# A local transformer's step loop: four quads of heads in flight in place of three, in a new order of phases

## Chip, core and metric

The kernel runs on one core of one Trainium2 chip. The metric is the device time of one launch in microseconds; lower is better. Times before the change are of three runs, and one further execution was profiled.

## What is computed

The reference is a chain of twelve residual blocks on an activation of 8 x 256 tokens by 128 channels, all in float32: expert layers, attentions, a recurrent block, and twice a six-layer local transformer (the reference's `_L2_ffn_ref`). The change touches only that transformer, which is run once before and once after another attention. Its core:

```python
def attn_layer(x, Wqkv, qs, ksc, Wo):           # 16 heads of 64
    q, k, v = split(x @ Wqkv)
    q = l2norm(q) * qs;  k = l2norm(k) * ksc
    q = q * cos * scale + rotate_half(q) * sin * scale
    k = k * cos * inv + rotate_half(k) * sin * inv
    out = local_attention(q, k, v)              # windows of 32, each sees itself and the one before
    return out @ Wo
def ffn_layer(x, g, bln, W1, b1, W2, b2):
    xn = layernorm(x) * g + bln
    a, gate = split(xn @ W1 + b1)
    return a * gelu(gate) @ W2 + b2
for i in range(6):
    x = attn_layer(shift_tokens(x), ...) + x
    x = ffn_layer(shift_tokens(x), ...) + x
```

`shift_tokens` moves the upper half of the channels by one token; `l2norm` divides each head's 64 values by their norm.

## The kernel before

Activations lie transposed, 128 channels on the partitions, in groups of two sequences (`T` = 512 tokens, four groups). The twelve stages follow one another; a local stage is `ffn2` (L1583). A **unit** is one layer for one group, 6 x 4 = 24 in a stage and 48 in the kernel. A unit has 16 heads in four **quads** of four heads, so a stage has 96 quads, and one pass of the loop in `ffn2`, a **step**, takes in one new quad `q0` while the ones of the steps before, `q1` and `q2`, are at later phases. Phases of a quad:

- `quad_project` (L1304): for k and then q, two matmuls into a pair of psum banks (`pp`); ScalarE squares it (`l_sq`), VectorE multiplies it with the sine table (`l_y`) and the cosine table (`l_yk`, `l_yq`); two DMAs swap neighbouring partitions (`l_yr`, L1318).
- `quad_norms` (L1335): the squares' column sums for q and k in one psum bank, four strips of 32 partitions; Ln and Exp on ScalarE give 1/norm (`l_rn`); two DMAs spread the key part over the partitions (`l_sq<-l_rn`, L1353); GpSimd adds the swapped half to k (`l_yk`).
- `quad_values` (L1323): the values (`vp`), copied by ScalarE to `l_v` and by two DMAs into a copy shifted by 32 rows (`l_w`).
- `quad_scale` (L1357): small matmuls turn the query norms into columns (`l_rq`, here called picks), VectorE adds the swapped half to q and multiplies k with its norms into the padded key rows (`l_kp`).
- `quad_scores` (L1376): mask and 64 small score matmuls (`sc`; 128 in the trace[...]), maximum and subtraction on VectorE (`l_mx`, `l_e`), multiplication with the query norms on GpSimd. `quad_exp` is ScalarE's Exp.
- `quad_turn` (L1412): transposes of `l_e`, copied by ScalarE to `l_at`. `quad_weigh` (L1422): two pairs of psum banks (`cx`) of weighted values, divided by VectorE (`l_cx`). `quad_back` and `quad_done`: transposes of `l_cx`, copied by ScalarE to `l_ct`.

When a unit's last quad is done, `local_rest` (L1461) does the remainder in pieces handed out four to a step by `piece`: the output projection in three parts, the residual sum `x1`, its shift `xs` (upper half on ScalarE, lower half on GpSimd), the layer norm, the gate matmuls with Gelu, the second matmul. A new unit's input is shifted the same way at the head of the step of its first quad.

Three things set the order. All instructions of VectorE, ScalarE, GpSimd and TensorE in the stage are forced into program order by `_Ordered` (their rows in the profile therefore all carry L298); DMAs are issued from SyncE. Psum: three pairs go round in turn for everything that `two` gives out, one bank for norms and picks (`bank`), one accumulator (`acc`). The buffers of `l_sq` are two, shared by k's squares, q's squares and the spread norms.

Of the kernel before, what the change touches and what calls it, by code (L numbers as in the profile page):

```python
# [21 lines left out]
F32 = mybir.dt.float32  # L22
# [6 lines left out]
P = 128  # L29
B, S, D = 8, 256, 128  # L30
NB = 2
# [275 lines left out]
class _Net:  # L307
# [98 lines left out]
    def spare(self):  # L406
        return self.bank.tile([P, T], F32, tag="bank", name="bank")

    def norm_parts(self, x, mean="mean", eps=0, gamma=None, beta=None, out=None, own=False):


        bank, tile = (self.ps, self.work) if own else (self.spare, self.scratch)
        m = bank()
        self.mm(m, self.get(mean), x)
        xc = tile("ln_c")
        self.nc.vector.tensor_tensor(xc, x, m, ALU.subtract)
        sq = tile("ln_sq")
        self.nc.scalar.activation(sq, xc, AF.Square)
        yield
        v = bank()  # L420
        self.mm(v, self.get(mean), sq)
        r = tile("ln_r")
        with self.reading(LN_EXP):
            self.rsqrt(r, v, eps, tile=tile)
        y = self.new_x() if out is None else out
        self.nc.vector.tensor_tensor(y, xc, r, ALU.mult)
        if gamma is not None:
            self.nc.vector.tensor_scalar(y, y, gamma, beta, ALU.mult, ALU.add)
        return y
# [871 lines left out]
            out[k] = t.unsqueeze(1).to_broadcast([P, 4, S])  # L1301
        return out

    def quad_project(self, q):  # L1304

        nc = self.nc
        four = lambda a: a.rearrange("p j (b s) -> p (j b) s", b=NB)
        for n, o in (("k", S), ("q", 0)):
            pp = self.two("pp")
            for j in range(2):  # L1310
                self.mm(pp[:, j, :], q.w[:, o + P * j : o + P * (j + 1)], q.xs)
            sq = self.work("l_sq", (P, 2, T), bufs=2)
            nc.scalar.activation(sq, pp, AF.Square)
            y2 = self.work("l_y2", (P, 2, T), bufs=2)
            nc.vector.tensor_tensor(four(y2), four(pp), q.tab[n + "sin"], ALU.mult)
            yr = self.work("l_yr", (P, 2, T), bufs=2)
            for a in range(2):
                nc.sync.dma_start(yr[a::2], y2[1 - a :: 2])  # L1318
            y = self.work("l_y" + n, (P, 2, T), bufs=2)
            nc.vector.tensor_tensor(four(y), four(pp), q.tab[n + "cos"], ALU.mult)  # L1320
            q.y[n], q.yr[n], q.sq[n] = y, yr, sq

    def quad_values(self, q):  # L1323
        nc = self.nc
# [10 lines left out]
    def quad_norms(self, q):  # L1335


        nc = self.nc
        sp = self.ps()
        for s, (n, j) in enumerate((("q", 0), ("q", 1), ("k", 0), ("k", 1))):  # L1340
            to, sq = sp[32 * s : 32 * s + 32, :], q.sq[n][:, j, :]
            if n == "k":
                self.mm(to, self.get("hsum"), sq)
                continue
            for b in range(NB):
                bs = slice(S * b, S * (b + 1))
                self.mm(to[:, bs], self.get("hsum"),
                        sq[:, bs].rearrange("p (c x i) -> p x c i", c=2, x=2))
        q.rn = self.work("l_rn", bufs=2)
        self.rsqrt(q.rn, sp, 2, scale=2.0**SH, shift=3)  # L1350
        q.rk = self.work("l_sq", (P, 2, T), bufs=2)
        for j in range(2):
            nc.sync.dma_start(q.rk[:, j, :], q.rn[64 + 32 * j : 96 + 32 * j, :].unsqueeze(1)  # L1353
                              .to_broadcast([32, 4, T]))
        nc.gpsimd.tensor_tensor(q.y["k"], q.y["k"], q.yr["k"], ALU.add)

    def quad_scale(self, q):  # L1357


        nc = self.nc  # L1360
        tp = self.ps()[:, :16].rearrange("p (m r) -> p m r", r=4)
        for b in range(NB):
            for x in range(2):
                o = S * b + P * x
                self.mm(tp[:, 2 * b + x, :], q.rn[:64, o : o + P], self.get("hpick")[:64, :])
        q.rq = self.work("l_rq", (P, 16), bufs=2)
        nc.vector.tensor_scalar(
            q.rq.rearrange("p (r m) -> p r m", m=4), tp.rearrange("p m r -> p r m"), 1e12, None,
            ALU.min)
        nc.vector.tensor_tensor(q.y["q"], q.y["q"], q.yr["q"], ALU.add)  # L1370
        q.kp = self.kp[q.n % 2]
        nc.vector.scalar_tensor_tensor(
            q.kp[:, :, WIN:], q.rk.rearrange("p j (b s) -> p (j b) s", b=NB), 1e12,
            q.y["k"].rearrange("p j (b s) -> p (j b) s", b=NB), ALU.min, ALU.mult)
# [86 lines left out]
    def local_rest(self, u):  # L1461


        nc, i = self.nc, u.i
        acc = self.accp.tile([P, T], F32, tag="acc", name="wo_acc")

        def project(cs):
            for c in cs:
                self.mm(acc, u.wo[:, c, :], u.ct[c // 2][:, c % 2, :], start=c == 0, stop=c == 7)

        project(range(3))
        yield False
        yield False
        project(range(3, 6))
        yield False
        project(range(6, 8))
        u.x1 = self.new_x()
        nc.vector.tensor_tensor(u.x1, acc, self.ys[u.g], ALU.add)
        xs = self.shifted(u.x1)
        yield False  # L1480

        self.settle()
        norm = self.norm_parts(xs, gamma=self.get(f"F{i}_ln_g"), beta=self.get(f"F{i}_ln_b"),
                               out=self.scratch("t", bufs=2))
        next(norm)
        for _ in range(3):
            yield True
        u.hn = yield from norm
        yield False

        o = self.accp.tile([P, T], F32, tag="acc", name="w2_acc")
        ags = []

        def second(m):
            f = GE_CHUNKS[m][1]
            self.mm(o, u.w2[:f, m, :], ags[m][:f, :], start=m == 0, stop=m == 2)

        def first(m):
            f, w = GE_CHUNKS[m]
            pp = self.two("ge")  # L1500
            self.mm(pp[:w, 0, :], u.w1[:, INNER + f : INNER + f + w], u.hn)
            self.mm(pp[:w, 1, :], u.w1[:, f : f + w], u.hn)
            gl = self.work("l_gl", bufs=2)
            self.act(gl[:w, :], pp[:w, 0, :], AF.Gelu, bias=self.get(f"F{i}_b1", 3 + m, 1)[:w, :])
            ag = self.work("l_ag", bufs=2)
            nc.vector.scalar_tensor_tensor(ag[:w, :], pp[:w, 1, :],
                                           self.get(f"F{i}_b1", m, 1)[:w, :], gl[:w, :],
                                           ALU.add, ALU.mult)
            ags.append(ag)

        self.table("gelu_and_others")
        first(0)
        yield True
        first(1)
        yield True
        second(0)
        yield True
        first(2)
        self.table(LN_EXP)
        second(1)  # L1520
        yield False

        yield False
        yield False
        yield False
        second(2)
        x2 = self.new_x()
        nc.vector.scalar_tensor_tensor(x2, o, self.get(f"F{i}_b2"), u.x1, ALU.add, ALU.add)
        self.ys[u.g] = x2
        if i == DEPTH - 1:  # L1530
            z = self.new_x()
            nc.vector.scalar_tensor_tensor(z, x2, 0.5, self.x[u.g], ALU.mult, ALU.add)
            self.finish(u.g, z)
        yield False
# [48 lines left out]
    def ffn2(self):  # L1583
# [2 lines left out]
        self.table(LN_EXP)  # L1586
        self.ys = [None] * NG
        gen = self.quads()
        q1 = q2 = None
        pieces, left = iter(()), 0  # L1590
        while True:
            q0 = next(gen, None)
            if not (q0 or q1 or q2 or left):
                break
            left = max(left - 1, 0)
            if q2 and q2.last:
                pieces, left = self.local_rest(q2.unit), 3
            if q1:
                self.quad_scores(q1)
            if q0:  # L1600
                self.quad_project(q0)
                if not q0.n:
                    self.window_rows()
            if q1:
                self.quad_exp(q1)
            if q2:
                self.quad_back(q2)
            if q0:
                self.quad_norms(q0)
            if q2:  # L1610
                self.quad_done(q2)
            if q0:
                self.quad_values(q0)
            self.piece(pieces)
            if q1:
                self.quad_turn(q1)
            self.piece(pieces)
            if q0:
                self.quad_scale(q0)
            self.piece(pieces)  # L1620
            if q1:
                self.quad_weigh(q1)
            self.piece(pieces)
            q1, q2 = q0, q1
        self.nc = real


# [136 lines left out]
```

## Time and profile before

| what | us |
|---|---|
| median of three runs | 5755.86 |
| lowest and highest run | 5738.87 and 5764.16 |
| the profiled execution's own time | 5764.6 |
| its span from first to last instruction | 5762.8 |
| local stages in it (960 to 2830, 3175 to 5060) | 3755 |
| TensorE busy in the span | 5194.9 |
| VectorE busy | 3389.1 |
| ScalarE busy | 2447.9 |
| GpSimd busy | 986.3 |

The mean granted TensorE clock of the profiled execution is 0.948 of full speed. In group rows the columns are line, engine, operation, output and inputs, count, then busy us and mean ns, then the engine's idle time just before. Matmuls overlap one another, so their durations do not add up; the distance from one start to the next does. In rows of waits the columns are who waited and for what, total us, number of times, longest. In rows of a stretch of time they are the stretch, its length, busy us of each engine with the number of instructions, the granted clock, the DMA engines' share and GB/s.

### The profile page before, as it was taken

Reading aid. Unit: us, or ns where it says so; the run is one execution under the profiler, and the core shown is the slowest. Engines: PE = TensorE matmul, PEld = TensorE weight load, DVE = VectorE, ACT = ScalarE, POOL = GpSimd, SP = SyncE. Lnnn points to the kernel's source line nnn. Section 1 sums busy time; section 2 is a strip of 40 time slices with the busy share of each in tenths; the row PEclk is TensorE's granted clock in tenths of the full one; section 3 lists DMA queues with packets and bytes.
Section 4 is the critical chain, followed back from the end, with each engine's and each line's share of the span. In section 5 each row is a group of like instructions: output and inputs, shape, how many; then the busy total and the mean of one; then the engine's idle time right before and its main releaser. Section 6 shows DMA issues by size and latency. Waiting matters only on the chain.

```text
span 5762.8 us, 160699 instructions
## 1 busy us (share of the span) xinstructions
PE 5194.9 (90%) x72688; PEld 3146.7 (55%) x72688; DVE 3389.1 (59%) x4903; ACT 2447.9 (42%) x2948; POOL 986.3 (17%) x627
## 2 busy tenths in 40 slices
PE   9989997898999999898888899899999999889889
PEld 6756754555555555555544455555555555555446
DVE  4444455666666666666635666666666666645555
ACT  2233235444444444444434344444444444432342
POOL 0000022222222222222200222222222222200000
PEclk9999988999999999999989899999999999989899
DMA  1000001344443434443300344344444444310000
GB/s 65 1 1 1 1 1 50 101 116 115 114 112 108 127 102 126 109 113 108 98 22 1 101 112 123 104 123 109 123 112 116 118 110 112 100 45 1 1 1 8
DMA packets 171995, 448.39 MB, mean 78 GB/s; under 512 B 26545, under 2 KB 40754, under 8 KB 171058
## 3 DMA queue, kind: packets, MB, share of 16 engines
q1 hardware_dynamic: 171314, 438.12, 27.7%
q8 instruction: 573, 9.39, 0.7%
q14 instruction: 108, 0.88, 0.0%
HBM read 45.51 MB, written 1.05 MB: 8 GB/s over the span
## 4 chain that ended last, share of the span: by engine, by line
PE 68%; ACT 10%; DMA 9%; DVE 8%; issue 4%; POOL 0%; SPq 0%; DVEq 0%; ACTq 0%; POOLq 0%
PE pp L298 14%; PE mm L353 10%; DMA l_sq<-l_rn 9%; PE bank L298 8%; PE e_o L353 6%; PE wo_acc L298 6%; PE ge L298 5%; PE sc L298 4%; ACT l_sq L298 3%; PE vp L298 3%; PE cx L298 3%; PE ms L298 3%; DVE l_kp L298 2%; ACT l_ct L298 2%; PE ss L298 2%
## 5 line engine op out<-in xcount | busy, mean ns | idle before, releaser
L298 ACT ACTIVATE l_sq<-pp 128x1024 f32<-128x1024 f32 x384 | 393.5, 1025 | 1106.2 <-PE pp L298 1106.2
L298 PE MATMUL pp<-l_xs,wqkv 128*128 128x512 f32 x1536 | 789.9, 661 | 11.1 <-ACT l_xs L298 6.6
L298 POOL TENSOR_TENSOR l_e<-l_e,l_rq 128x1024 f32<-128x1024 f32 x192 | 365.6, 1904 | 1881.1 <-DVE l_e L298 1705.7
L298 POOL TENSOR_TENSOR l_yk<-l_yk,l_yr 128x1024 f32<-128x1024 f32 x192 | 452.6, 2357 | 615.6 <-DMA l_yr<-l_y 571.5
L298 PE MATMUL sc<-l_kp,l_yq 64*32 64x64 f32 x24576 | 329.7, 247 | 222.4 <-DVE l_kp L298 200.0
L298 PEld LDWEIGHTS pp<-l_xs,wqkv 128*128 128x128 f32 x1536 | 309.6, 213 | 362.8 <-issue 337.3
L353 PE MATMUL mm<-x,m 128*128 128x512 f32 x1024 | 479.1, 608 | 0.0
L298 PEld LDWEIGHTS sc<-l_kp,l_yq 64*32 64x32 f32 x24576 | 284.0, 115 | 284.4 <-DVE l_kp L298 225.4
L298 DVE SCALAR_TENSOR_TENSOR l_kp<-l_sq,l_yk 128x1024 f32<-128x1024 f32 x192 | 234.7, 1222 | 307.7 <-DMA l_sq<-l_rn 307.5
L353 PEld LDWEIGHTS e_o<-m,e_h 128*128 128x128 f32 x3072 | 362.9, 192 | 60.6 <-issue 60.1
L298 PE MATMUL vp<-wqkv,l_xs 128*128 128x256 f32 x1536 | 382.4, 392 | 1.8 <-PE bank L298 1.1
L298 PE MATMUL wo_acc<-l_ct,wo 128*128 128x512 f32 x768 | 365.3, 609 | 0.0
L353 PE MATMUL e_o<-m,e_h 128*128 128x128 f32 x3072 | 363.5, 275 | 0.0
L298 PEld LDWEIGHTS vp<-wqkv,l_xs 128*128 128x128 f32 x1536 | 276.0, 189 | 114.9 <-issue 77.7
L298 PE MATMUL cx<-l_w,l_at 64*32 64x65 f32 x12288 | 285.5, 228 | 47.1 <-ACT l_at L298 39.3
L298 DVE TENSOR_TENSOR l_y<-pp,l_ksin 128x1024 f32<-128x1024 f32 x192 | 234.8, 1223 | 154.6 <-ACT l_sq L298 154.4
L298 PEld LDWEIGHTS cx<-l_w,l_at 64*32 64x32 f32 x12288 | 251.7, 106 | 129.6 <-issue 80.2
L298 DVE TENSOR_REDUCE l_mx<-sc 128x16 f32<-128x1024 f32 x192 | 234.5, 1221 | 121.6 <-PE sc L298 120.2
L298 PE MATMUL cx<-l_v,l_at 64*32 64x65 f32 x12288 | 290.4, 228 | 11.5 <-issue 11.5
L353 PEld LDWEIGHTS mm<-x,m 128*128 128x128 f32 x1024 | 190.0, 195 | 197.5 <-issue 170.7
L298 PE MATMUL ge<-t,w 128*128 128x512 f32 (+1 forms) x576 | 281.3, 612 | 12.6 <-DVE t L298 5.7
L298 ACT ACTIVATE lv<-bank,sb_c 128x512 f32<-128x512 f32 x268 | 183.8, 686 | 239.1 <-PE bank L298 233.7
(277 smaller groups left out, 9202.4 us busy)
## 6 DMA issues: line engine op xcount, KB each, us to landing
l_yr<-l_y SPq DMA_DIRECT2D x768, 256.0 KB, 2.4
l_sq<-l_rn SPq DMA_DIRECT2D x384, 256.0 KB, 4.3
l_w<-l_v SPq DMA_DIRECT2D x192, 390.0 KB, 6.3
wqkv<-in_f_wqkv SPq DMA_DIRECT2D x48, 384.0 KB, 4.5
l_w<-l_v SPq DMA_DIRECT2D x192, 65.0 KB, 5.5
wo<-in_f_wo SPq DMA_DIRECT2D x12, 512.0 KB, 3.3
m<-in_m_w SPq DMA_DIRECT2D x16, 256.0 KB, 5.4
w<-in_f_w SPq DMA_DIRECT2D x12, 341.0 KB, 2.8
```

The lines of the kernel that those rows point to most:

```text
L298: r = f(*args, **kw)
L353: self.nc.tensor.matmul(out, lhsT=lhsT, rhs=rhs, start=start, stop=stop)
```

## The change

A fourth quad, `q3`, is in flight: the context is turned back and copied a step after it was weighed. `quad_scale` becomes `quad_keys` and runs at the head of the step after the quad's norms. The phases of a step stand in a new order, k's and q's projections are called apart, and the four places of a piece lie elsewhere. The query norms are taken on the tokens' own order, and the picks put them into window order with twice as many matmuls of half the columns. The layer norm inside `local_rest` uses the accumulator's bank, and the pieces are spread anew.

| order in a step | |
|---|---|
| before | scores q1, project k and q q0, exp q1, back q2, norms q0, done q2, values q0, piece, turn q1, piece, scale q0, piece, weigh q1, piece |
| after | keys q1, project k q0, exp q2, project q q0, piece, turn q2, back and done q3, weigh q2, piece, norms q0, piece, scores q1, values q0, piece |

```diff
     def quad_norms(self, q):
...
         for s, (n, j) in enumerate((("q", 0), ("q", 1), ("k", 0), ("k", 1))):
-            to, sq = sp[32 * s : 32 * s + 32, :], q.sq[n][:, j, :]
-            if n == "k":
-                self.mm(to, self.get("hsum"), sq)
-                continue
-            for b in range(NB):
-                bs = slice(S * b, S * (b + 1))
-                self.mm(to[:, bs], self.get("hsum"),
-                        sq[:, bs].rearrange("p (c x i) -> p x c i", c=2, x=2))
+            self.mm(sp[32 * s : 32 * s + 32, :], self.get("hsum"), q.sq[n][:, j, :])
...
-    def quad_scale(self, q):
+    def quad_keys(self, q):
...
             for x in range(2):
-                o = S * b + P * x
-                self.mm(tp[:, 2 * b + x, :], q.rn[:64, o : o + P], self.get("hpick")[:64, :])
+                for c in range(2):
+                    o = S * b + P * c + 64 * x
+                    self.mm(tp[64 * c : 64 * c + 64, 2 * b + x, :], q.rn[:64, o : o + 64],
+                            self.get("hpick")[:64, :])
...
     def local_rest(self, u):
...
         project(range(3))
         yield False
-        yield False
         project(range(3, 6))
         yield False
+        yield False
+
         project(range(6, 8))
         u.x1 = self.new_x()
         nc.vector.tensor_tensor(u.x1, acc, self.ys[u.g], ALU.add)
         xs = self.shifted(u.x1)
         yield False
-
+        yield False
         self.settle()
         norm = self.norm_parts(xs, gamma=self.get(f"F{i}_ln_g"), beta=self.get(f"F{i}_ln_b"),
-                               out=self.scratch("t", bufs=2))
+                               out=self.scratch("t", bufs=2), bank=self.bank1)
         next(norm)
-        for _ in range(3):
-            yield True
+        yield True
+        yield True
+
         u.hn = yield from norm
         yield False
+        yield False
...
         self.table("gelu_and_others")
         first(0)
-        yield True
         first(1)
-        yield True
-        second(0)
         yield True
         first(2)
         self.table(LN_EXP)
+        second(0)
         second(1)
         yield False
 
-        yield False
-        yield False
-        yield False
         second(2)
...
     def ffn2(self):
...
+            if q1:
+                self.quad_keys(q1)
+            if q0:
+                self.quad_project(q0, "k")
+                if not q0.n:
+                    self.window_rows()
+            if q2:
+                self.quad_exp(q2)
+            if q0:
+                self.quad_project(q0, "q")
+            self.piece(pieces)
+            if q2:
+                self.quad_turn(q2)
+            if q3:
+                self.quad_back(q3)
+                self.quad_done(q3)
+                if q3.last:
+                    pieces, left = self.local_rest(q3.unit), 4
+            if q2:
+                self.quad_weigh(q2)
+            self.piece(pieces)
+            if q0:
+                self.quad_norms(q0)
+            self.piece(pieces)
             if q1:
                 self.quad_scores(q1)
             if q0:
...
                 self.quad_values(q0)
             self.piece(pieces)
...
-            q1, q2 = q0, q1
+            q1, q2, q3 = q0, q1, q2
```

## What I predicted before seeing the result

> **What bounds the kernel now.** I read the page first: TensorE is busy 90% of the span, but its clock row shows 8s and 9s, and the chain that ended last holds 9% of a DMA, the key norms' broadcast.
>
> ```profile
> span 5762.8 us, 160699 instructions
> PE 5194.9 (90%) x72688; PEld 3146.7 (55%) x72688; DVE 3389.1 (59%) x4903; ACT 2447.9 (42%) x2948; POOL 986.3 (17%) x627
> PEclk9999988999999999999989899999999999989899
> PE pp L298 14%; PE mm L353 10%; DMA l_sq<-l_rn 9%; PE bank L298 8%; PE e_o L353 6%; PE wo_acc L298 6%; PE ge L298 5%; PE sc L298 4%; ACT l_sq L298 3%; PE vp L298 3%; PE cx L298 3%; PE ms L298 3%; DVE l_kp L298 2%; ACT l_ct L298 2%; PE ss L298 2%
> ```
>
> Then the stage windows of the two local stages, the only ones touched:
>
> ```profile
> 960.00:2830.00 1870.00, 1677.50 (x29593) 1010.49 (x29592) 1185.68 (x1433) 862.97 (x996) 429.12 (x245) 0.94 0.41 113
> 3175.00:5060.00 1885.00, 1688.24 (x30500) 1024.51 (x30498) 1207.01 (x1461) 873.44 (x1003) 436.44 (x244) 0.96 0.42 113
> ```
>
> Columns are length, busy PE, PEld, DVE, ACT, POOL, granted clock. They make 3755 us for 48 units of four steps: 78.2 us a unit. TensorE idles 192.5 + 196.8 = 389 us, 8.1 a unit. The clock is granted at 1.00 or 0.50, so a mean of 0.94 and 0.96 is half clock for 12% and 8%: 375 us; half of that is lost, 3.9 a unit.
>
> Then the chain in order of time, for one step:
>
> ```profile
> 2043.92 1.03 ACT l_sq L298
> 2044.99 1.16 PE bank L298 x8
> ...
> 2046.23 0.70 ACT lv L298
> ...
> 2048.68 5.81 DMA l_sq<-l_rn
> ...
> 2054.58 1.22 DVE l_kp L298
> ```
>
> Within one step: square, norm matmuls, Ln, Exp, broadcast DMA, scaled keys; then the scores can start. From the norms' end to the keys takes 8.3 to 9.5 us in eight steps of ten (2046.07 to 2054.58 here). The waits name it, and two waits on residual sums of which the change moves one:
>
> ```profile
> PE sc L298 <- DVE l_kp L298: 200.0, 85, 3.9
> DVE l_kp L298 <- DMA l_sq<-l_rn: 307.5, 132, 4.0
> POOL l_xs L298 <- DVE x L298: 461.4, 48, 23.1
> ACT l_xs L298 <- DVE x L298: 311.3, 48, 6.8
> ```
>
> **The change, part by part.** I lay TensorE's matmuls of one step end to end, start to start, at full clock: picks 0.98, k and q projections 3.51, turns of e 0.87, turns of context 0.88, weigh 1.42, norms 1.0, scores with mask 1.73, values 1.83: 12.2. Pieces per unit: Wo 16 x 0.43, two norm means 0.86 each, gate and up 12 x 0.45, W2 6 x 0.49: 16.9. A unit is 4 x 12.2 + 16.9 = 65.9, and 65.9 + 8.1 + 3.9 = 77.9 meets the 78.2. The change leaves this work nearly alone, so all turns on idle time and clock.
>
> *What it removes.* Keys wait a step, so the chain above leaves the scores: up to 200 us. The norm matmuls no longer wait for the squares (about 0.24 a step, 46 us).
>
> *What it puts there.* Three psum pairs go round, each step takes eight (k, q, turned e, turned context, weigh 0 and 1, scores, values), so weigh 0 needs q's pair back, read last by DVE. This is the timeline of DVE from k's square on:
>
> ```profile
> 2043.26 1.22 DVE L298 TENSOR_TENSOR l_y<-pp,l_ksin 128x1024 f32<-128x1024 f32 x1 [0.49 <-ACT l_sq L298]
> 2044.40 1.21 DVE L298 TENSOR_TENSOR l_yk<-pp,l_kcos 128x1024 f32<-128x1024 f32 x1
> 2045.53 1.21 DVE L298 TENSOR_TENSOR l_y<-pp,l_qsin 128x1024 f32<-128x1024 f32 x1
> 2046.66 1.21 DVE L298 TENSOR_TENSOR l_yq<-pp,l_qcos 128x1024 f32<-128x1024 f32 x1
> ```
>
> k's projection starts at 2040.18, q's pair is free at 2047.87: 7.7 us. Before, TensorE filled them with q, context turns, norms and values. Now only projections (3.5) and two turns (1.75) lie there, so weigh starts 1.0 + 7.7 = 8.7 into the step (idle 2.4, less a piece), and 1.42 + 1.0 + 1.73 + 1.83 = 6.0 follow: 14.7 plus later pieces. A unit's four steps I call A (Wo), B (sum and mean), C (variance and gate), D (last W2):
>
> - D: 14.7; TensorE work 13.2, idle 1.5.
> - A: D has no piece after its norms, so D's norms end 3.6 us before A starts. Keys start 8.3 after that (the quick end, the swaps having landed), at 4.75; the four DVE reads queue behind them at 1.13 spacing, q's pair is free at 10.5, weigh starts there: 10.5 + 6.0 + 5.14 of Wo = 21.7; work 17.4, idle 4.3.
> - B: the sum x1 (0.69) stands behind yq on DVE and ends at 9.3; the ACT half of the shift (0.61) waits for it with l_at (1.0) queued behind, so weigh starts at 11.0: 11.0 + 6.0 + 0.86 = 17.85; work 14.8, idle 3.05. Before, this shift ended a step, with nothing urgent behind it.
> - C: a new unit's input shift heads the step, and its POOL half stands behind the score multiply of B, now late in its step: scores end 1.8 before C starts, then max 1.25, subtraction 1.22, multiply 1.90, shift 0.60 on POOL: projections start at 3.5 and not 1.0. 14.7 + 2.5 + 7.4 of pieces = 24.6; work 20.5, idle 4.1.
>
> Idle: 4.3 + 3.05 + 4.1 + 1.5 = 12.95 against 8.1.
>
> *Clock.* Half clock comes in stretches of 3.41 us; the first row is the stretch before one, the second the slow one:
>
> ```profile
> 2014.67:2018.08 3.41, 1.05 (x89) 0.89 (x96) 2.97 (x6) 0.00 (x0) 0.00 (x0) 1.00 0.38 105
> 2018.08:2021.49 3.41, 3.41 (x67) 1.79 (x51) 2.97 (x3) 0.00 (x0) 0.00 (x0) 0.50 0.02 5
> ```
>
> 2.36 us of idle there were enough. Over both stages every such stretch with 2 us idle or more was followed by a slow one, few below 1.4. [...] By the trace, A's gaps (2.1 and 1.4 with turns between) trip it nearly always, B's 2.95 in three of four, C's 2.5 in six of ten, at 1 to 2 us each: 3.65 a unit, as much as before. I take the trace: 65.9 + 12.95 + 3.65 = 82.5.
>
> *Picks, eight matmuls where four were (16 against 8 in the trace).* Before: 8 in 0.98, 188 ns a load of 128 columns. Halves load 64 columns into two column groups; the weigh row runs 128 small ones in 1.42. From below 0.5, from above 1.96 if each costs as before[...]. I take 1.0 (half the columns, twice the count); 1.96 adds about 1 in B and D, +94 us; 0.5 gives -48.
>
> *At nothing.* Query norm matmuls on 512 columns: same columns, 1.0 (0.9 to 1.07). Norms' means in the accumulator bank: wo, mean, variance, w2 follow one another anyhow. Exp moved ahead of q's square on ACT: 1.06, with q's DVE reads not due before (their slack 0.6 before; 0.15 now); if it is late, q's pair is late with it. Gelu pieces pulled together: the table loads (1.28) lie beside 7.4 us of TensorE work. DMAs: k's swap, q's swap, norm broadcast, values keep their order on SP; values' copy has two steps of slack; the broadcast now leaves before the value copy and after the swaps landed, so 7.6 (the least seen) to 9.5: -34 to +58 us. POOL's key add has a step. One step more to drain: some 5 us a stage.
>
> **Sum.** (82.5 - 78.2) x 48 = +206 on the profiled execution's 5764.6, which lies 8.7 over the median of the runs: 5755.9 + 206 = 5962, said as 5960.
>
> **Rivals.**
> 1. *Slower, as above*: chance 0.60; own range 5860 to 6080 (picks, broadcast, clock 2 to 5.5 a unit).
> 2. *Faster*: A's, B's and C's three queue waits are hidden, since one of the orders is not what I read. Idle is then 2.45 + 0.75 + 1.6 + 1.5 = 6.3, no stretch trips the clock often (1.0): 73.2, -5.0 x 48 = -240: 5515; with one of the waits left some 5620. For it: 200 us of score waits do go. Against: each wait is an in-order queue. Chance 0.22. It turns where the three waits fall from 6.7 to 2.4 us a unit.
> 3. *A wash*: the same waits, but gaps broken by the turns keep the clock up: +31, 5785; a wait less, 5730. Chance 0.08 within 0.5%.
> 4. *Slower still*: slow stretches feed themselves (after a slow one, 0.5 us idle kept it slow more often than not) and the picks cost double: 6 a unit of clock and +2: 5962 + 113 + 94 = 6170. Chance 0.10.
>
> A measurement of this kernel tells about 0.5%. So faster 0.22, same 0.08, slower 0.70. The range 5610 to 6080 takes in rival 3 and the near end of rival 2; rival 4's end and the best of rival 2 stay out.
>
> **What would show it.** Right: waits of PE sc for l_kp gone; PE cx waiting for DVE l_yq and for ACT l_at; PE pp waiting for POOL l_xs some 2.5 us in 46 steps or so; DVE l_kp still waiting for the broadcast in one step of four; TensorE idle near 620 us in the local stages at a clock of 0.93 to 0.96. Wrong: weigh starting within 7 us of a step's start, projections never waiting for the shift, or a clock of 0.99.

## The result, and the profile after

| | before | after |
|---|---|---|
| median of the runs, us | 5755.59 (5738.87 to 5764.16, 4 runs) | 6125.86 (6124.63 to 6129.66, 4 runs) |
| span of the profiled execution, us | 5762.8 | 6127.7 |
| mean granted TensorE clock | 0.948 | 0.932 |

The time after is 1.0648 times that before, with a 95% interval of 1.0624 to 1.0673: 370 us more. The direction was forecast and the size was not: +206 was expected, and the result lies above the range of 5610 to 6080.

These are four lines of the page of the changed kernel: span, busy times, the clock in 40 slices, and the chain that ended last by line.

```profile
span 6127.7 us, 162271 instructions
PE 5232.1 (85%) x73456; PEld 3059.9 (50%) x73456; DVE 3698.7 (60%) x4903; ACT 2467.4 (40%) x2947; POOL 1079.8 (18%) x627
PEclk9999988998999998999989899999999999899999
PE mm L353 9%; PE pp L298 8%; PE bank L298 7%; PE e_o L353 6%; PE sc L298 6%; PE ge L298 4%; PE wo_acc L298 4%; DVE l_y L298 4%; PE cx L298 4%; DVE l_yq L298 3%; DVE l_mx L298 2%; DVE l_yk L298 2%; DVE l_e L298 2%; PE ms L298 2%; POOL l_e L298 2%
```

The broadcast of the key norms, 9% of the chain before, is gone from its costliest lines (all DMAs together are 1% of the chain now). In its place stand VectorE lines that were not among them: `l_y`, `l_yq`, `l_mx`, `l_yk`, `l_e`. VectorE runs the same 4903 instructions in 310 us more busy time, which no step of the prediction has.

These are the stage windows again, of the kernel before and then of the changed one, drawn so that they hold both local stages whole. The two shown with the prediction ended 106 and 43 us before the stages did, so its 78.2 us a unit was too low: read from step to step, a unit took 79.0.

```profile
964.00:2936.00 1972.00, 1760.38 (x30720) 1055.79 (x30720) 1229.93 (x1493) 903.13 (x1045) 440.74 (x245) 0.94 0.40 109
3174.00:5103.00 1929.00, 1720.50 (x30688) 1039.77 (x30688) 1217.44 (x1477) 886.75 (x1021) 439.05 (x248) 0.95 0.41 110
```

```profile
964.00:3118.00 2154.00, 1774.61 (x31103) 1010.13 (x31104) 1379.57 (x1493) 913.22 (x1045) 490.46 (x245) 0.92 0.35 100
3362.00:5467.00 2105.00, 1742.21 (x31071) 998.11 (x31072) 1376.79 (x1477) 897.29 (x1019) 482.32 (x248) 0.93 0.35 101
```

The stages grew from 3901 to 4259 us: 358 of the 365 us by which the span grew. TensorE's idle time in them went from 420 to 742 us (+322). The clock records show it at half clock for 417 us before and 647 us after. TensorE was at work in 354 and 523 us of these, and half of that is lost (the projections' matmuls start 429 ns apart at full clock and 853 ns at half): 177 and 262 us (+85). What is left, 3304 and 3255 us, is work at full clock (-49). The forecast had +233 of idle, -12 of clock and no saving; these make 221, and its 206 comes of taking off 78.2 a unit where its own terms for before made 77.9. The forecast took half of all half-clock time as lost, idle time within it included; counted so, the clock's part is +115.

Read by the type of step, from the first pick of one step to that of the next, means in us (they move by up to 0.3 with the number of steps left out at a stage's ends):

| step | predicted at full clock | measured length | idle, predicted | idle, measured | time at half clock |
|---|---|---|---|---|---|
| D | 14.7 | 16.4 | 1.5 | 2.3 | 1.0 |
| A | 21.7 | 21.2 | 4.3 | 2.6 | 1.0 |
| B | 17.85 | 20.8 | 3.05 | 4.0 | 4.55 |
| C | 24.6 | 28.0 | 4.1 | 5.7 | 5.3 |
| a unit | 78.85, with clock 82.5 | 86.4 | 12.95 | 14.6 | 11.8 (9.7 of it at work, so 4.9 lost) |

Taken in the same way, a unit before was 78.95 with 7.85 of idle and 6.9 at half clock (3.0 lost). Most of the clock loss sits in B and C, the two steps in which a shift waits.

The longest waits of TensorE and one of VectorE, in the changed kernel ("issue" is time in which the engine waited for nothing that the profile shows):

```profile
PE pp L298 <- POOL l_xs L298: 194.1, 47, 4.8
...
PE cx L298 <- ACT l_at L298: 186.2, 95, 3.4
...
PE ct L298 <- DVE l_yk L298: 92.8, 91, 2.3
...
PE cx L298 <- issue: 55.5, 59, 1.9
...
DVE l_kp L298 <- DMA l_sq<-l_rn: 24.7, 35, 3.3
```

No row of PE sc waiting for `l_kp` is left. The two costliest rows are the two shifts that the prediction named: the input shift ahead of the projections (4.1 us each, where 2.5 was forecast) and `l_at`, which stands on ScalarE behind the shift of `x1` (155.6 of the 186.2 us fall in the 47 steps B).

Why 4.1 and not 2.5 is seen in three groups, of the kernel before and then of the changed one:

```profile
L298 POOL TENSOR_TENSOR l_e<-l_e,l_rq 128x1024 f32<-128x1024 f32 x192 | 365.6, 1904 | 1881.1 <-DVE l_e L298 1705.7
...
L298 DVE TENSOR_TENSOR l_yq<-l_yq,l_yr 128x1024 f32<-128x1024 f32 x192 | 234.9, 1223 | 2.3 <-DMA l_yr<-l_y 2.3
...
L298 DVE SCALAR_TENSOR_TENSOR l_kp<-l_sq,l_yk 128x1024 f32<-128x1024 f32 x192 | 234.7, 1222 | 307.7 <-DMA l_sq<-l_rn 307.5
```

```profile
L298 POOL TENSOR_TENSOR l_e<-l_e,l_rq 128x1024 f32<-128x1024 f32 x192 | 417.6, 2175 | 1623.5 <-DVE l_e L298 1410.0
...
L298 DVE TENSOR_TENSOR l_yq<-l_yq,l_yr 128x1024 f32<-128x1024 f32 x192 | 364.6, 1899 | 1.3 <-issue 1.1
...
L298 DVE SCALAR_TENSOR_TENSOR l_kp<-l_sq,l_yk 128x1024 f32<-128x1024 f32 x192 | 299.2, 1559 | 25.2 <-DMA l_sq<-l_rn 24.7
```

They now run at the same time. The timeline of VectorE and then of GpSimd at the head of one step C (start, duration) shows what happens:

```profile
2258.94 1.22 DVE L298 TENSOR_TENSOR l_yq<-l_yq,l_yr 128x1024 f32<-128x1024 f32 x1
2260.70 2.30 DVE L298 SCALAR_TENSOR_TENSOR l_kp<-l_sq,l_yk 128x1024 f32<-128x1024 f32 x1 [0.54 <-DMA l_sq<-l_rn]
```

```profile
2259.01 2.91 POOL L298 TENSOR_TENSOR l_e<-l_e,l_rq 128x1024 f32<-128x1024 f32 x1 [7.51 <-DVE l_e L298]
2261.86 1.60 POOL L298 COPY l_xs<-x 64x512 f32<-64x512 f32 x1
```

The query sum starts first and runs at its own 1.22 us; the score multiply beside it takes 2.91, which is 1.0 more than alone. Then the keys start under the multiply and take 2.30, ending some 1.1 us after it; and the shift that starts behind the multiply ends 0.46 us after the keys do, and takes 1.60 where 0.61 is its time alone. Each time the later one ends as if it had stood until the earlier one was done; this is the exclusion spoken of below. It is so throughout: the 136 query sums and key scalings that start under the multiply or the shift end 1.08 to 1.20 us after it, however much of it was left; the 52 multiplies and 36 shifts that come second end 1.76 and 0.47 us after the VectorE instruction. The next two rows are the windows of this step's head and of what follows:

```profile
2258.17:2263.50 5.33, 0.63 (x17) 0.54 (x16) 4.28 (x4) 1.62 (x2) 4.46 (x2) 0.99 0.51 133
2263.50:2268.70 5.20, 5.18 (x9) 2.31 (x10) 0.50 (x1) 1.53 (x2) 0.00 (x0) 0.69 0.00 0
```

TensorE does its picks (0.6 us), stands for 4.7 us, and then runs 5.2 us at a mean clock of 0.69. The wait is paid once as idle time, and again as 1.6 us of lost clock (0.31 of 5.2).

### The profile page after: what moved, and what is told of

Read it like the earlier page. It is cut to its first block, busy times and chain, and to the rows that moved or that the text cites. A ratio compares the mean times of both kernels' runs of the same rounds, so it can differ in the third digit from the quotient of the medians.

```text
span 6127.7 us, 162271 instructions
## 1 busy us (share of the span) xinstructions
PE 5232.1 (85%) x73456; PEld 3059.9 (50%) x73456; DVE 3698.7 (60%) x4903; ACT 2467.4 (40%) x2947; POOL 1079.8 (18%) x627
## 3 DMA queue, kind: packets, MB, share of 16 engines
q1 hardware_dynamic: 171314, 438.12, 24.7%
## 4 chain that ended last, share of the span: by engine, by line
PE 61%; DVE 22%; ACT 7%; issue 6%; POOL 3%; DMA 1%; SPq 0%; DVEq 0%; POOLq 0%; ACTq 0%
PE mm L353 9%; PE pp L298 8%; PE bank L298 7%; PE e_o L353 6%; PE sc L298 6%; PE ge L298 4%; PE wo_acc L298 4%; DVE l_y L298 4%; PE cx L298 4%; DVE l_yq L298 3%; DVE l_mx L298 2%; DVE l_yk L298 2%; DVE l_e L298 2%; PE ms L298 2%; POOL l_e L298 2%
## 5 line engine op out<-in xcount | busy, mean ns | idle before, releaser
L298 POOL TENSOR_TENSOR l_e<-l_e,l_rq 128x1024 f32<-128x1024 f32 x192 | 417.6, 2175 | 1623.5 <-DVE l_e L298 1410.0
L298 PE MATMUL cx<-l_w,l_at 64*32 64x65 f32 x12288 | 346.7, 245 | 244.3 <-ACT l_at L298 186.2
L298 ACT COPY l_v<-vp 128x1024 f32<-128x1024 f32 x192 | 194.4, 1012 | 635.9 <-PE vp L298 565.9
L298 PEld LDWEIGHTS cx<-l_w,l_at 64*32 64x32 f32 x12288 | 278.5, 115 | 308.0 <-ACT l_at L298 216.0
L298 ACT ACTIVATE lv<-bank,sb_c 128x512 f32<-128x512 f32 x221 | 151.9, 687 | 685.4 <-PE bank L298 685.4
L298 PE MATMUL cx<-l_v,l_at 64*32 64x65 f32 x12288 | 354.6, 245 | 24.6 <-issue 24.6
L298 DVE TENSOR_TENSOR l_yq<-l_yq,l_yr 128x1024 f32<-128x1024 f32 x192 | 364.6, 1899 | 1.3 <-issue 1.1
L298 PE MATMUL sc<-l_kp,l_yq 64*32 64x64 f32 x24576 | 302.8, 227 | 34.3 <-issue 34.3
L298 DVE SCALAR_TENSOR_TENSOR l_kp<-l_sq,l_yk 128x1024 f32<-128x1024 f32 x192 | 299.2, 1559 | 25.2 <-DMA l_sq<-l_rn 24.7
L298 PE MATMUL ct<-sb_c,l_cx 128*128 128x128 f32 x1536 | 218.5, 289 | 102.6 <-DVE l_yk L298 92.8
```

The lines of the kernel that those rows point to most:

```text
L298: r = f(*args, **kw)
```

## The experiments

All ratios are to the kernel before, run beside it on the same chip. Differences in us from the changed kernel are between medians taken on different chips; the medians of the kernel before on these lie between 5751 and 5760 us. The letter Q in the expectations is the theory that a queue order (an instruction standing behind another on its engine) sets the loss; the other theories are named there.

**1. The input shift of a new unit, one step earlier.** This is the changed kernel with the shift issued before the last quad of the unit ahead of it is handed out, so that it has the rest of a step to finish. A fourth `l_xs` buffer is needed, for which the tables lose their second one; what that costs by itself was not run.

```diff
-        self.xs = [one("l_xs", i, (P, T)) for i in range(3)]
+        self.xs = [one("l_xs", i, (P, T)) for i in range(4)]
...
-            t = self.work("l_" + k, (P, S), bufs=2)
+            t = self.work("l_" + k, (P, S), bufs=1)
...
-                xs = self.shifted(self.ys[g])
+                xs = self.unit_input(i, g) if (i, g) == (0, 0) else ahead
...
+                    if c == 3 and i * NG + g + 1 < DEPTH * NG:
+                        ahead = self.unit_input(*divmod(i * NG + g + 1, NG))
                     yield q
```

> The changed kernel, but a new unit's input is shifted one step earlier (a fourth l_xs buffer; the table tiles get one buffer each to make room). Theory Q (waits in in-order queues, my prediction's C term): the projections' wait for POOL l_xs, 194 us in 47 steps, goes, and the slow clock that follows it; step C falls from 28.0 to about 22.5 us, 48 x 5.5 = -260: about 5870 us. Rival R (the rotation of three psum pairs is the bound): the wait reappears at weigh as a wait for q's pair, C falls by 2 at most: about 6030 us.

Measured: 5938.4 us (5934.07 to 5945.37), ratio 1.0316 [1.0296, 1.0337], 187 us under the changed kernel. The group of the projections no longer waits for it:

```profile
L298 PE MATMUL pp<-l_xs,wqkv 128*128 128x512 f32 x1536 | 715.4, 609 | 4.3 <-DMA wqkv<-in_f_wqkv 3.1 <-POOL l_xs L298 1.1 <-issue 0.2
```

Step C fell from 28.0 to 23.9 us, and half clock from 11.8 to 8.1 us a unit. No wait at weigh came in its place in C, but a shorter one did: the context's turns wait for `l_yk`, the reader of k's psum pair, 46 times there and 1.5 us each, where they hardly did in the changed kernel. So the rival named above is right in part: a third of the wait comes back at the psum pairs, without the slow clock.

**2. The sum `x1` and its shift, one place earlier.** They now stand at the last place of A instead of the first of B, so nothing urgent is queued behind them on ScalarE.

```diff
         project(range(3, 6))
         yield False
-        yield False
 
         project(range(6, 8))
...
         yield False
         yield False
+        yield False
         self.settle()
```

> The changed kernel, but the third part of the output projection with x1 and its shift stands at the last place of step A in place of the first of step B. Theory Q (B term): the wait of weigh for l_at behind the shift, about 2.4 us in step B, goes, and most of that step's 4.5 us of slow clock; 48 x 3.5 = -170: about 5955 us. Rival R: weigh waits for q's pair at nearly the same point, 48 x 1 = -50: about 6075 us.

Measured: 5945.83 us (5943.0 to 5949.07), ratio 1.0328 [1.0309, 1.0348], 180 us under the changed kernel. The row of waits for `l_at` falls from 186.2 us in 95 to:

```profile
PE cx L298 <- ACT l_at L298: 36.7, 51, 3.0
```

B fell from 20.8 to 15.4 us, while A took over its piece (21.2 to 23.0); B's half clock went from 4.55 to 0.08 us.

**3. Both at once.** The edits of 1 and 2 together.

> The changed kernel with both earlier edits: a new unit's input shifted a step earlier, and x1 with its shift at the last place of step A. If the two waits are separate queues, the gains add: 6126 - 188 - 180 = about 5758 us. If they share one cause (q's psum pair behind them, or the clock), less than three quarters of the sum comes: above 5850 us.

Measured: 5757.82 us (5749.4 to 5763.12, 12 runs), ratio 0.9997 [0.9985, 1.0009]. The two effects add up (187 + 180 = 367; 368 measured), and the net loss is gone: a unit is 78.6 us with 9.4 of idle and 3 at half clock. So two places in the queues cost as much as the whole change loses, and what else it gains and costs comes out even. VectorE and GpSimd still exclude each other here (the multiply takes 2.19 us, the shift 1.53).

**4. Small query-norm matmuls alone, on the kernel before.** Only the query norms as single matmuls, and the halved picks.

```diff
-            to, sq = sp[32 * s : 32 * s + 32, :], q.sq[n][:, j, :]
...
+            self.mm(sp[32 * s : 32 * s + 32, :], self.get("hsum"), q.sq[n][:, j, :])
...
-                self.mm(tp[:, 2 * b + x, :], q.rn[:64, o : o + P], self.get("hpick")[:64, :])
+                for c in range(2):
+                    o = S * b + P * c + 64 * x
+                    self.mm(tp[64 * c : 64 * c + 64, 2 * b + x, :], q.rn[:64, o : o + 64],
+                            self.get("hpick")[:64, :])
```

> The kernel before, with the small query-norm matmuls alone. Picks fall from 0.98 to about 0.6 us. If that counts only where TensorE is the bound (two steps of four): 96 x 0.4 = -40: about 5715 us. If the chain of the key norms hides it all: 5750 us. If the small matmuls cost TensorE more than they save: above 5770 us.

Measured: 5776.06 us (5766.08 to 5786.31, 10 runs), ratio 1.0037 [1.0024, 1.0049]. The long steps get shorter, but the time does not follow. The four kinds of step before were 24.2, 15.9, 23.3 and 15.6 us; now the two long ones, full of TensorE work, are 23.1 and 22.3, and the two short ones, which have few pieces to fill them, 17.2 and 16.9. The wait for the keys did shrink (from 200.0 to 146.4 us), but weigh waits more (on issue 112.3 us for 19.3, on `l_at` 76.7 for 39.3). Half clock rose from 6.9 to 9.8 us a unit. What goes with the waits on issue is said under experiment 9.

**5. Keys between the projections: an attempt to part VectorE from GpSimd.** VectorE's two instructions of the keys step, the query sum and the key scaling, go behind k's two reads, so that they no longer meet the score multiply.

```diff
+    def quad_keys_sum(self, q):
...
         nc.vector.tensor_tensor(q.y["q"], q.y["q"], q.yr["q"], ALU.add)
...
                 self.quad_exp(q2)
+            if q1:
+                self.quad_keys_sum(q1)
             if q0:
                 self.quad_project(q0, "q")
```

> The changed kernel, but VectorE's two sums of the keys step (q with its swapped half, k with its norms) run after k's two reads of psum and before q's. Theory S (VectorE instructions with two SBUF inputs and GpSimd exclude each other at the head of the step): the l_yq sum falls from 1.90 to 1.22 us, l_kp from 1.56 to 1.22, the score multiply from 2.18 to 1.90, the projections' wait for POOL l_xs from 4.1 to about 2.5 us, and A's broadcast wait goes: about 6000 us. Rival: the slow instructions lie beside other work and q's pair is free no sooner: 6100 to 6130 us.

Measured: 6581.15 us (6578.43 to 6582.63), ratio 1.1431 [1.141, 1.1452]: 455 us slower than the changed kernel, which neither theory expected. The parting itself worked: `l_yq` takes 1216 ns, `l_e` 1913, and the projections wait for the shift 2.7 us each time (127.3 us in 47), the size that the prediction had. But the spread norms that the keys read lie in one of `l_sq`'s two buffers. While they wait there, q's square has no buffer, and everything behind it on VectorE waits. Two waits and one row of ScalarE's timeline of this kernel:

```profile
DVE l_y L298 <- ACT l_sq L298: 904.0, 382, 7.5
...
PE cx L298 <- ACT l_at L298: 763.9, 190, 6.8
```

```profile
2529.71 1.02 ACT L298 ACTIVATE l_sq<-pp 128x1024 f32<-128x1024 f32 x1 [3.79 <-issue]
```

**6. The same with a buffer of its own for the spread norms.** Beside the edit of 5 (the tables lose their second buffer here too):

```diff
-        q.rk = self.work("l_sq", (P, 2, T), bufs=2)
+        q.rk = self.work("l_rk", (P, 2, T), bufs=1)
```

> The changed kernel with both sums of the keys step between k's and q's reads, as in the run that took 6581 us, but the spread key norms have a buffer of their own and do not share l_sq's two. If that run was slow because q's square waits for l_kp to free the shared buffer, and l_at and weigh stand behind it: q's reads are still 2.3 us later than in the changed kernel, the exclusion is gone: 6150 to 6300 us. If the shared buffer plays no part: about 6580 us.

Measured: 6028.13 us (6025.17 to 6041.61), ratio 1.0486 [1.0458, 1.0515], 553 us under experiment 5. The shared buffer was what had cost there. What is left still delays q's reads: `l_at` holds weigh for 273.4 us (97 times).

**7. The query sum alone moved away from the score multiply.** It goes into the quad's own norms phase, after weigh, where GpSimd is not in the multiply.

```diff
         nc.gpsimd.tensor_tensor(q.y["k"], q.y["k"], q.yr["k"], ALU.add)
+        nc.vector.tensor_tensor(q.y["q"], q.y["q"], q.yr["q"], ALU.add)
...
     def quad_keys(self, q):
...
-        nc.vector.tensor_tensor(q.y["q"], q.y["q"], q.yr["q"], ALU.add)
```

> The changed kernel, but VectorE's sum of q with its swapped half runs in the quad's own norms phase, after the weighing of the step and not at the head of the next; no buffer or wait of another instruction changes. Theory S (VectorE with two SBUF inputs and GpSimd exclude each other): the sum falls from 1.90 to about 1.22 us, the score multiply from 2.18 towards 1.9, the projections' wait for POOL l_xs from 4.1 to about 3 us: 48 x 1.1 plus some slow clock, about 6050 us. Rival: the exclusion lies beside other work: 6110 to 6140 us.

Measured: 5968.32 us (5950.9 to 5994.29), ratio 1.037 [1.0325, 1.0415], 158 us under the changed kernel: twice what was expected. Both groups are nearly at their own lengths again, though the keys now start under the multiply more often (1782 ns):

```profile
L298 DVE TENSOR_TENSOR l_yq<-l_yq,l_yr 128x1024 f32<-128x1024 f32 x192 | 239.2, 1246 | 80.9 <-DMA l_yr<-l_y 80.7
...
L298 POOL TENSOR_TENSOR l_e<-l_e,l_rq 128x1024 f32<-128x1024 f32 x192 | 367.3, 1913 | 1601.8 <-DVE l_e L298 1293.6 <-DVE l_rq L298 234.7 <-ACT l_v L298 31.1
```

The wait of the projections for the shift fell from 4.1 to 3.4 us (158.2 in 47), and A, B and C each got about 1 us shorter. But the move also takes 1.2 us out of the head of VectorE's queue, so this run alone does not say whether the exclusion or the shorter queue gave the 158 us.

**8. A stand-in in the place of the sum.** Beside the edit of 7, an instruction of the same length that reads psum stands where the query sum had been: the older quad's subtraction once more, into a buffer that nothing reads (for which the tables lose their second one).

```diff
+        if old:
+            stand_in = self.work("l_in", (P, 2 * T), bufs=1)
+            nc.vector.tensor_tensor(stand_in.rearrange("p (n k) -> p n k", k=64), old.sv, old.mx,
+                                    ALU.subtract)
         q.kp = self.kp[q.n % len(self.kp)]
...
-                self.quad_keys(q1)
+                self.quad_keys(q1, q2)
```

> The changed kernel with the query sum moved as in the run before (158 us gained), and in its old place at the head of VectorE's row an instruction of the same length that reads psum (the subtraction of the older quad's scores once more, into a buffer that nothing reads). VectorE's queue is then as long as in the changed kernel, but nothing at that place has both operands in SBUF. Theory X (the gain came from the score multiply on GpSimd no longer meeting the sum): most of the gain stays, 5970 to 6020, the multiply at about 1.9 us, the projections' wait for the shift near 3.4 us. Theory L (it came from a row of VectorE that is one instruction of 1.2 us shorter ahead of the psum reads): the gain is gone, 6100 to 6140, whatever the multiply takes. Between them both have a part, in proportion.

Measured: 5953.1 us (5938.92 to 5962.15), ratio 1.035 [1.033, 1.0369]: 173 us under the changed kernel, with VectorE's queue as long as in it. So the gain does not come from a shorter queue; it comes from what stands beside GpSimd's multiply. The groups of this kernel:

```profile
L298 POOL TENSOR_TENSOR l_e<-l_e,l_rq 128x1024 f32<-128x1024 f32 x192 | 365.3, 1903 | 1589.2 <-DVE l_e L298 1542.5 <-ACT l_gl L298 27.3 <-ACT l_v L298 19.5
...
L298 DVE SCALAR_TENSOR_TENSOR l_kp<-l_sq,l_yk 128x1024 f32<-128x1024 f32 x192 | 289.6, 1508 | 42.1 <-DMA l_sq<-l_rn 35.1 <-POOL l_e L298 5.2 <-issue 0.5
...
L298 DVE TENSOR_TENSOR l_in<-sc,l_mx 128x1024 f32<-128x1024 f32 x190 | 230.7, 1214 | 0.0
```

The stand-in reads psum and takes 1214 ns beside the multiply, which takes its own 1903. It even puts the keys off until the multiply is nearly done (1508 ns in place of 1782 in experiment 7).

**9. Norms and a piece ahead of weigh.** A test of the pair wait: if weigh waits for a psum pair, work put ahead of it should fill the wait.

```diff
-            if q2:
-                self.quad_weigh(q2)
-            self.piece(pieces)
             if q0:
                 self.quad_norms(q0)
             self.piece(pieces)
+            if q2:
+                self.quad_weigh(q2)
+            self.piece(pieces)
             if q1:
                 self.quad_scores(q1)
```

> The changed kernel, but the norms of q0 and the piece after weigh stand ahead of weigh. Theory Q (A term and the pair): the norm matmuls (1.0 us) fill the wait for q's psum pair, and the spread norms leave about 2.4 us earlier, so A's wait of VectorE l_kp for the broadcast goes: 1 us in most steps and 1.5 in A, 192 x 0.8 + 48 x 1 = -200: about 5925 us. Rival (VectorE is the bound of the front half, whatever TensorE does there): 6080 to 6130 us.

Measured: 6089.5 us (6075.01 to 6102.07), ratio 1.0579 [1.0548, 1.061]: 36 us gained where some 200 were expected. The waits at weigh did shrink (`l_at` from 186.2 to 109.9 us), but the scores now often follow weigh directly, and stop within their run for a cause that the profile calls issue:

```profile
PE sc L298 <- issue: 129.0, 102, 3.4
```

It was 34.3 us in 45 in the changed kernel and 22.2 in 31 before. Of the 129 us, 103 fall in the 49 steps in which the scores follow weigh directly. The DMA records show what goes with these stops. This is the row of one queue in the page of the changed kernel (packets, MB, share of the DMA engines' time):

```profile
q8 instruction: 578, 9.47, 0.6%
```

Its packets are of 16 KB. Of the 102 stops of experiment 9, 101 end between 1.2 and 1.6 us after such a packet, and so do all 45 of the changed kernel's; of moments taken at random 5% do, and of weigh's 174 waits with a named releaser in the changed kernel none. Weigh's waits on issue go with these packets as well (59 of 59 in the changed kernel, 44 of 48 in experiment 4). Why TensorE stops there was not shown, and no run varied it by itself.

**10. Experiments 1, 2 and 9 together, with the query sum behind weigh.**

> The changed kernel with all four edits: input shift a step earlier, x1 and shift at the last place of A, norms ahead of weigh, q's sum after weigh. If the waits are separate and the slow clock goes with them: 65 us of TensorE work a unit plus some 6 idle and 2 of clock, 48 x (73 - 79) = -290 against before: about 5470 us. If only the two tested waits can be had: about 5750 us.

Measured: 5779.84 us (5755.53 to 5793.26, 20 runs), ratio 1.0032 [1.0019, 1.0045], where 5470 was expected. With the two shift waits gone the order of experiment 9 gains nothing and costs: issue in the scores rises to 163.7 us in 122 waits, 121 of which end behind a packet of that queue as above. It is 1.7% slower than experiment 11, in which norms and weigh keep their order.

**11. Experiments 1, 2 and 7 together.**

> The changed kernel with three edits: input shift a step earlier, x1 with its shift at the last place of A, q's sum in the norms phase after weigh. If the exclusion between VectorE and GpSimd cost time only through the projections' wait for the input shift, which the first edit has taken away, nothing more comes: about 5758 us. If it also lengthens VectorE's queue at the head of the other steps (A fell by 0.85 and B by 1.2 us with that edit alone): 48 x 2 = -96: about 5660 us.

Measured: 5673.42 us (5671.46 to 5684.5, 4 runs), ratio 0.9866 [0.9844, 0.9888]. This version beats the changed kernel and, by 1.3%, the one before. By the ratios it is also 1.3% (some 75 us) under experiment 3, which holds everything but the moved sum. So what the exclusion costs lies in part at other places than the two shifts; the price of the shifts (367 us) and that of the exclusion (158 us with the shifts in place) overlap and must not be added. Lines of its page, its windows of the first local stage, and its group of the query sum:

```profile
span 5673.4 us, 162200 instructions
PE 5073.1 (89%) x73456; PEld 2986.1 (53%) x73456; DVE 3558.8 (63%) x4903; ACT 2461.7 (43%) x2947; POOL 1039.2 (18%) x629
```

```profile
964.00:2892.00 1928.00, 1691.63 (x31107) 972.44 (x31108) 1313.74 (x1497) 911.06 (x1046) 473.14 (x247) 0.98 0.39 112
```

```profile
L298 DVE TENSOR_TENSOR l_yq<-l_yq,l_yr 128x1024 f32<-128x1024 f32 x192 | 240.6, 1253 | 113.1 <-DMA l_yr<-l_y 112.7
```

A unit is 76.9 us, with 8.3 of idle and 1.8 at half clock; the clock in the stage is 0.98 where it was 0.94 before. The two kernels idle about as long (7.85 before), but here in shorter pieces: gaps of 2 us and more make 0.6 us of a unit's idle time, where they made 3.7 before, and the time at half clock fell from 6.9 to 1.8 us.

**12. The new quad's values between q's projection and the turns, on top of 11.** It was meant to fill what is left of the wait before weigh.

```diff
                 self.quad_project(q0, "q")
+            if q0:
+                self.quad_values(q0)
...
                 self.quad_scores(q1)
-            if q0:
-                self.quad_values(q0)
```

> The kernel of the three edits, but the values' matmuls (1.83 us) stand between q's projection and the turn of e, where TensorE waits for psum pairs. If they fill that wait: 1 us a step, -190 against the three edits: about 5500 us. If the scores, now last in their step, make Exp late at the head of the next (sum, maximum, multiply and Exp are 5.5 us), or Exp and the copies queue up: no better than the three edits, 5660 to 5800 us.

Measured: 6601.28 us (6593.28 to 6608.89), ratio 1.1475 [1.145, 1.15]. The values have two buffers, and in this order the new quad's are written into the ones that weigh is about to read; so this kernel weighs the newer quad's values, and weigh waits for that step's own shifted copy. Its row of waits:

```profile
PE cx L298 <- DMA l_w<-l_v: 695.0, 184, 5.5
```

It says nothing of whether the wait could be filled; that stays open.

## Why the prediction was right, and where it was wrong

*Right: which waits go and which come.* The scores' wait for the keys is gone. Weigh waits for `l_at` behind the shift of `x1`, and the projections for GpSimd's half of the input shift (47 times; 46 were forecast). Experiments 1 to 3 show that these two cost as much as the net loss: with both shifts moved, 0.9997.

*B: right in kind, under-sized.* Weigh waits behind the shift of `x1` as foreseen, in 47 of 48 steps. But B idles 4.0 us for 3.05 (3.3 with the query sum moved, so most of the miss is the exclusion), and its clock was taken at 1 to 2 us in three cases of four and cost 2.0.

*C: under-sized.* The step "scores end, then max 1.25, subtraction 1.22, multiply 1.90, shift 0.60 on POOL: projections start at 3.5" took the durations of before. In the changed order VectorE's query sum and key scaling stand just where the multiply and the shift run, and they exclude each other: the multiply took 2.91 and the shift 1.60 in the step shown, and the wait was 4.1 us in place of 2.5. The idle time of C was 5.7, not 4.1. Experiments 7 and 8 show the exclusion and its price: with the sum moved away from the multiply the kernel gains 158 us, and with a psum-reading instruction put in its place it still gains 173. Experiments 5 and 6, in which the keys do not meet the multiply, give the wait as 2.7 us.

The step did not ask what the two engines do to each other side by side. The trace of before had hardly a case of it (6 of 192 query sums met a GpSimd instruction, the longest for 0.33 us, and no key scaling did), so nothing in its mean durations warned. In the changed kernel 132 of 192 query sums meet one (2.21 us where the others take 1.22), and 56 of the key scalings (2.40 against 1.21). VectorE instructions that read psum kept their 1.21 us beside GpSimd (109 of q's 192 cosine products met one). The view to take for a moved instruction is what GpSimd does at its new place, and not its mean in the old one.

*The clock: under-sized, the largest single term, and put in the wrong steps.* The step "3.65, as much as before" expected A to trip it in nine cases of ten. A, with turns between its gaps, spent only 1.0 us at half clock. B and C, each with one wait of 3 to 5 us, took 4.55 and 5.3. In the forecast's own count, half of all half-clock time, 5.9 us a unit were lost in place of 3.65. What it read from the trace of before (all 46 full-clock stretches of 3.41 us with 2.0 us of idle and more were followed by one at half clock, and 4 of the 932 with less than 1.4) held: in the changed kernel's stages all 81 with 2.0 us and more were followed by one at half clock, half of the 88 with 1.4 to 2.0 us, and none of the 888 with less; after a slow one, 0.6 us of idle kept it slow in 62 cases of 63.

*A: over-sized.* The step "keys start 8.3 after that" let the broadcast set the keys in one step of four. They waited for it 35 times, 24.7 us in all; weigh started 8.5 us into A where 10.5 was forecast, and the idle time was 2.6 us in place of 4.3.

*D and the pair wait: at another place.* The sign "PE cx waiting for DVE l_yq" did not come: no row of waits shows it. The wait for a psum pair stands one phase earlier, where the context's turns wait for k's reader `l_yk` (92.8 us in 91, in A and B). Weigh's second pair waits for ScalarE's `l_ct` (24.6 us in 79) and on issue (55.5 us in 59). D came out at 16.4 for 14.7; the waits on issue in its scores and weigh, some 1.0 us a step, were not foreseen.

*The picks: cheaper than taken.* Taken as 1.0, they measured 0.56 us in place of 0.98 a step, close to the lower end 0.5. The upper end of 1.96, each at its price of before, was far off. But as experiment 4 shows, that saving with the single norm matmuls makes the kernel before 0.4% slower.

*The sum.* Between forecast and result lie 159 us (365 against 206). In the forecast's own terms, a unit idled 1.65 us more than taken and lost 2.25 us more of clock, which for 48 units is 187 us; the base of 78.2 in place of 78.95 takes 36 of them back, and some 8 are left to the stages' ends. In that count its work of 65.9 us came out (86.4 - 14.6 - 5.9), while for the unit before its terms had made 77.9 where 78.95 was measured. The exclusion alone is of the right size for the whole miss: 158 and 173 us by experiments 7 and 8, its idle time and the clock that this costs taken together. With it out the kernel takes 5968 and 5953 us, where 5960 was forecast. But the terms still differ there (in experiment 7 idle 12.15 for 12.95, clock 4.5 for 3.65), so that the misses nearly cancel is luck and not foresight. The range had reached to 5.5 us of clock a unit, but not to that together with longer waits. In the rivals, "slower still" came near the size (6170) with one reason right (6 a unit of clock) and one wrong (double picks).

## What to carry to other kernels

Before moving an instruction on VectorE or GpSimd, look at what the other of the two does at the new place: here two instructions with all operands in SBUF took 2.2 to 2.9 us where 1.2 to 1.9 is their own time. A small copy that others wait for (here a shift of 0.6 us) belongs a place before the long instructions of its queue: two such copies cost as much as the whole 6.5% loss, and two small edits and a buffer undid it. And price an idle gap at its length plus half of the busy half-clock time that follows it: in the step C shown, 4.7 us of idle and 1.6 us of lost clock.

## What the runs showed of the hardware that I had not expected

- The exclusion of VectorE and GpSimd (multiplies of 1.90 us that came second took 2.80 to 2.98): it also acts on a small GpSimd copy (1.60 us in place of 0.61), the one of the two that starts first keeps its own time (1.22 us for the sum, 1.90 for the multiply), and a VectorE instruction that reads psum is free of it (1214 ns beside a multiply of 1903).
- TensorE: 16 picks that each load 64 columns took 0.56 us in the changed kernel, 35 ns each, where 8 that load 128 columns took 0.98 before.
- Where the scores' 128 small float32 matmuls follow weigh's 128 directly, they stop within their run: 103 us in 49 steps of experiment 9. In all, the scores stop for 129.0 us in 102 waits there and for 163.7 in 122 in experiment 10. 101 and 121 of these stops end 1.2 to 1.6 us after a packet of the queue `q8`; the cause was not shown.
- Taking TensorE work away can lengthen the kernel: in experiment 4 the two long steps became 1.0 and 1.1 us shorter, yet the unit spent 2.9 us more at half clock, and the time rose by 0.4%.
